# Five quarters of an MLP's second matmul by seven products in place of eight, inside the attention blocks of a Trainium2 kernel

## The chip, the cores and the metric

The kernel runs on one core of one Trainium2 chip. The metric is the device time of one execution in microseconds (us); less is better. A core has a matmul engine (PE, with a weight loader PEld), a vector engine (DVE), a scalar engine (ACT), GpSimd (POOL), DMA queues of which SP issues most, a working memory (SBUF) and eight accumulator banks (PSUM) of 128 x 512 f32 that PE writes and DVE and ACT read.

## The reference

A pre-norm transformer block with cross attention and an MLP: B = 4 sequences of L = 512 rows, D = 512, 16 heads, all in f32.

```python
q = (layer_norm(x, ln1) @ q_w + q_b)          # heads of 32
k, v = enc @ k_w + k_b, enc @ v_w + v_b
attn = softmax(where(mask, q @ k.T * scale, min))
hidden = (attn @ v) @ cproj_w + cproj_b + x
y = gelu(layer_norm(hidden, ln2) @ fc_w + fc_b)   # 512 -> 2048
out = hidden + y @ proj_w + proj_b                # 2048 -> 512
```

The change is in the last line, in `y @ proj_w` of the sequences 0 and 1.

## The kernel before

**Blocks.** Attention goes by 16 groups of four heads (w; four groups for each sequence b = w // 4) and by two halves of the query rows, which makes 32 blocks, p = 0 to 31. A block (`block`, L337) computes eight score tiles on PE (L317), which take all eight banks; DVE adds the mask and finds the minimum (`soften`, L323), ACT takes the exponential (L327), DVE transposes (L335, L360). POOL copies (L393) and DMAs on SP's queue (L398) exchange the transposed blocks between partitions (`copies`). Ahead of block p's scores, `attend` multiplies block p − 2 with V on PE (L415), and DVE divides by the sums of the rows as it takes the result out (oT, L420). The bank of that product is the last that the next eight score tiles get.

**Fills.** PE would be idle while DVE and ACT do the softmax, so each block has a list of other matmul work (`put(p, ...)`, L1115 to L1164): the projections of later groups (k, q, v), the cproj of a finished sequence, and the MLP's two matmuls of the sequences 0 and 1. `fill(0)` comes after the softens, `fill(1)` after the last transpose, each up to a budget of 3.4, and `fill(2)` issues what is left. `put` is written by hand; every engine executes its instructions in the order in which the program issues them (`manual_schedule`). `mid=` places work between the two sets of softens, and work that costs 0 (`do`) holds loads, sums and norms of other engines.

**The MLP.** fc goes by pairs of column chunks, each by seven products after Strassen and Winograd instead of eight (`fc_seven`, L634), with sums of weight blocks made on POOL (`fc_sums`, L679). proj goes by quarters (b, q): four of the 16 chunks of the inner dimension for all 512 rows. Before the change a quarter is four parts (`proj`, L701), one for each 128 rows: four matmuls 128x512 into one bank (L705), and one DVE addition of the bank to the residual tile (L709). PE shows each f32 matmul as two records. Six quarters are done this way: (0,0) to (0,3), (1,0) and (1,1). The rest of sequence 1 and the sequences 2 and 3 are done behind the blocks in `last_mlps` (L737), where proj goes by seven products already. `some(n)` takes the next items of the list `products` (L571): an fc pair counts 2, a part of proj 1. Before, (0,0) is in block 15, (0,1) in 19 and 20, (0,2) in 23 and 26, (0,3) in 27 and 28, (1,0) in 30 and 31, and (1,1) after block 31, between pieces of the last sequence's cproj (`cproj_last`, L460, itself by seven products, L479).

**Banks and buffers.** `acc_tile` (L119) hands out the eight banks in turn. An instruction that takes a bank waits for its last reader. `mlp_w` (L96) gives eight slots to the weights of fc and proj, which `load_mlp` (L582) refills as parts are done. The weights of k, q and v have two slots each in `ptt` (`kqv_w`, L111).

**After block 31** (L1184 on): `attend` of block 30, the last cproj's products q1c and q2c between parts of (1,1), stats and norms of sequence 2, POOL's row additions (`c_bias`, L437), `attend` of block 31, the rest of (1,1), then q6c, q3c, q5c and q4c, sums of proj's weights (`p_sums`, L731), and the fc pairs (1,4) to (1,7) in `last_mlps`.

Of the kernel before, what the change touches and what calls it, by code (L numbers as in the profile page):

```python
# [34 lines left out]
FIRST = 2  # L35
IN_G = (1, 3, 5, 7)
IN_XE = (25, 27, 29, 31)

BY_ROW = ((1, 1), (1, 3))
BY_ACT = ((1, 2),)  # L40
# [11 lines left out]
def xattn_block(ctx: ExitStack, tc: tile.TileContext, x, rawT, encT, mask, q_w, k_w, v_w, c_w, fc_w, p_w, vecs, rows, out):  # L52
# [6 lines left out]
    const, keep, hids, tiles, small = pools(ctx, const=1, keep=1, hids=4, tiles=4, small=4)  # L59
# [28 lines left out]

    ys = const.tile([P, 3, 2, L // 2], F32, tag="ys", name="ys")
    wsum = const.tile([P, 2, 3, 2, P], F32, tag="wsum", name="wsum")  # L90

    def k_q(w, i):
        n = w % 4 * 2 + i
# [15 lines left out]
        return ptt[:, n * D : (n + 2) * D]  # L109

    def kqv_w(w, i):  # L111
        n = 4 * i + 2 + w % 2
        return ptt[:, n * D : (n + 1) * D].rearrange("p (d f) -> p d f", d=ND)

    S = {"gelu": []}
# [92 lines left out]
            )  # L208

    def load_rn(b):  # L210
        S["rows", b] = [hids.tile([P, L], F32, tag="hid2", bufs=2, name=f"rn_{b}_{i}") for i in range(2)]
# [28 lines left out]
    def load_w(w, queue=None, names=("wk", "wq", "wv")):  # L240
# [4 lines left out]
        for i, (n, src) in enumerate((("wk", k_w), ("wq", q_w), ("wv", v_w))):  # L245
            if n in names:
                S[n, w] = kqv_w(w, i)
                (queue or Q[0]).dma_start(out=S[n, w], in_=src[:, g, :, :])

    def prep_k(w):  # L250
        b, g = divmod(w, NG)
        kT = k_q(w, 0)
        acc = acc_tile(f"acck_{w}")
        for d in range(ND):
            nc.tensor.matmul(acc, S["wk", w][:, d, :], eT[:, d, :], start=(d == 0), stop=(d == ND - 1))  # L255
        load_w(w + 2, names=("wk",))
        nc.scalar.activation(kT, acc, AF.Identity, bias=vec[:, KB + g : KB + g + 1], scale=1.0)
        S["kT", w] = kT

    def prep_q(w):  # L260
        b, g = divmod(w, NG)
        qT = k_q(w, 1)
        parts = [slice(0, L)] if w else [slice(0, 2 * P), slice(2 * P, L)]
        for c in parts:
            acc = acc_tile(f"accq_{w}_{c.start}")[:, c]
            for d in range(ND):
                nc.tensor.matmul(acc, S["wq", w][:, d, :], xT[:, d, c], start=(d == 0), stop=(d == ND - 1))  # L267
            nc.scalar.activation(qT[:, c], acc, AF.Identity, bias=qb[:, g : g + 1], scale=-scale)
        load_w(w + 2, names=("wq",))
        S["qT", w] = qT  # L270

    def prep_v(w):
# [159 lines left out]
    def load_h(b, *ts_):  # L432

        if ("xa", b) not in S:
            S["xa", b] = dram.tile([L, D], F32, tag=f"xa{b}", name=f"xa{b}")
        for t in ts_:
            if b == B - 1:  # L437

                S["h", b, t] = k_q(t // 2, t % 2)
            else:  # L440
                pool, tag, n = (tiles, "xn", 4) if not stays(b, t) else (hids, "hid2", 2) if b else (hids, "hid", 4)
                S["h", b, t] = pool.tile([P, D], F32, tag=tag, bufs=n, name=f"h_{b}_{t}")
# [93 lines left out]
    def load_hid(b, ts_):  # L536

        for t in ts_:
            if ("hid", b, t) not in S:
                S["hid", b, t] = hids.tile([P, D], F32, tag="hid", name=f"hid_{b}_{t}")  # L540
# [24 lines left out]
    def fcs(b, *cs):  # L565
        return [("fc", b, c) for c in cs]

    def pjs(b, q, *ts_):
        return [("p", b, q, t) for t in ts_ or range(NT)]

    products = fcs(0, 0, 1, 2, 3) + pjs(0, 0) + fcs(0, 4, 5) + pjs(0, 1) + fcs(0, 6, 7) + pjs(0, 2)  # L571
    products += fcs(SPLIT, 0) + pjs(0, 3) + fcs(SPLIT, 1, 2, 3) + pjs(SPLIT, 0) + pjs(SPLIT, 1)
    last_use, done = {}, 0
    for name, b, i, *_ in products:
        n = 2 if name == "fc" else FQ
# [6 lines left out]
    def load_mlp():  # L582

        while count[0] < len(weights) and (count[0] < MW or weights[count[0] - MW][3] < count[1]):
            name, b, f, _ = weights[count[0]]
            w = mlp_w(count[0])
            if name == "fc":
                w = w.rearrange("p (d f) -> p d f", d=ND)
            Q[0].dma_start(out=w, in_=fc_w[:, f, :, :] if name == "fc" else p_w[ts(f, P), :])
            S[name + "w", b, f] = w  # L590
            count[0] += 1

    NP = NF // 2
# [104 lines left out]
        count[4] += 1  # L698
        load_mlp()

    def proj(b, q, t):  # L701
        gelus(q % 2)
        acc = acc_tile(f"accp_{b}_{q}_{t}")
        for k in range(FQ):
            nc.tensor.matmul(  # L705
                acc, gT[q % 2][:, k, ts(t, P)], S["pw", b, q * FQ + k], start=(k == 0), stop=(k == FQ - 1)
            )
        h = S["hid", b, t]
        nc.vector.tensor_tensor(h, acc, h, ALU.add)  # L709
        if q == NQ - 1:  # L710
            (nc.gpsimd if b == 0 else nc.sync).dma_start(out=out[b, ts(t, P), :], in_=h)
# [25 lines left out]
    def last_mlps():  # L737
# [197 lines left out]
        for b, pairs, new in (  # L935
# [43 lines left out]

            project(b, pairs, sums, turns, middle)  # L980
            if b == SPLIT:
                S["more"] = [hids.tile([P, D], F32, tag="hid2", bufs=2, name=f"more_{n}") for n in range(2)]
                S["more"] = [m.rearrange("p (c n) -> p c n", c=NP // 2) for m in (*S["more"], row[:, 2, :])]
                to_split.extend(w_sums(5, pt[:, 2]))


# [86 lines left out]
    def some(n):  # L1073
# [4 lines left out]
        assert n == 0  # L1078
        return taken

    def hid_(b, *ts_):
        return do(lambda: load_hid(b, ts_))

# [20 lines left out]
    def put(p, *work, before=(), mid=()):  # L1104
# [48 lines left out]
    put(22, [k, q], norm(1, 0, 1), some(2), norm(1, 2, 3))  # L1153
    k15, q15, _ = A(15)
    put(23, some(1), [k15], t2, pb_(1), some(1), h_(2, 2, 3, 0, 1))
# [93 lines left out]
```

## Time and profile before

| | |
|---|---|
| median of three runs | 760.17 us (759.89 to 760.55) |
| the profiled execution, and its span | 760.67 us, 758.9 us |
| PE, DVE, ACT, POOL busy | 753.9, 613.4, 337.6, 339.7 us |
| granted clock of PE | 0.999 |

The span runs from the first instruction to the last; the execution's time has 1.8 us around it. In the rows of the profile, a group of instructions has the line of `before.py` (L705), the engine, the operation, what is written and read by the program's names, the shape, the count, busy us and mean ns of one, and the idle time ahead of them with what ended it. Rows of the timeline begin with the start in us and the duration; those of the windows with the stretch and its length, and then give each engine's busy time.

### The profile page before, as it was taken

To read this page: it belongs to the slowest core of one execution; us is meant where nothing else is said; L and a number is where in the kernel's file an instruction comes from. 1 tells how busy PE (TensorE), PEld (TensorE's weight loads), DVE (VectorE), ACT (ScalarE), POOL (GpSimd) and SP (SyncE) were. 2 spreads that over 40 slices of the span, in tenths; PEclk is the share of its full clock that TensorE was granted. 3 is DMA by queue.
4 is the path that set the end of the run, shared out by engine and by line. 5 is a ranking of instruction groups with operands and counts; after the bars stand their busy time and mean duration, and the time that the engine had idled before them with its cause. 6 is when DMAs were issued, how large, how long until landed. Compare 5 with 4: busy or idle time off the path is not lost.

```text
span 758.9 us, 13040 instructions
## 1 busy us (share of the span) xinstructions
PE 753.9 (99%) x4418; PEld 517.8 (68%) x4418; DVE 613.4 (81%) x1222; ACT 337.6 (44%) x768; POOL 339.7 (45%) x352
## 2 busy tenths in 40 slices
PE   9999999999999999999999999999999999999998
PEld 6655555567574545475454566468888899988997
DVE  3889999879995777887887989949877986956865
ACT  2566766565873574647753567501302221022200
POOL 1549447368664873244575444432050004403153
PEclk9999999999999999999999999999999999999999
DMA  9989889467897776665756867776724402046001
GB/s 329 341 255 247 207 207 257 104 199 200 220 243 229 223 231 177 184 175 129 177 133 186 214 194 193 172 227 215 260 98 135 167 26 91 30 146 214 1 15 43
DMA packets 60577, 134.59 MB, mean 177 GB/s; under 512 B 11312, under 2 KB 17072, under 8 KB 60384
## 3 DMA queue, kind: packets, MB, share of 16 engines
q1 hardware_dynamic: 58448, 126.73, 58.4%
q0 software_dynamic: 1920, 7.01, 2.7%
q8 instruction: 35, 0.57, 0.3%
q14 instruction: 30, 0.25, 0.1%
q10 hardware_dynamic: 144, 0.02, 0.0%
HBM read 69.23 MB, written 11.02 MB: 106 GB/s over the span
## 4 chain that ended last, share of the span: by engine, by line
PE 99%; POOL 0%; issue 0%; DVE 0%; DVEq 0%; POOLq 0%
PE q L646 26%; PE accp L705 11%; PE r L792 10%; PE sc L317 8%; PE av L415 8%; PE acck L255 8%; PE accq L267 8%; PE accc L455 6%; PE accv L278 5%; PE accv L298 3%; PE q1p L853 2%; PE tp L166 1%; PE warm L1044 1%; PE q3p L835 0%; PE q5p L835 0%; PE q4p L835 0%
## 5 line engine op out<-in xcount | busy, mean ns | idle before, releaser
L327 ACT ACTIVATE ptt<-ptt,mn 128x512 f32<-128x512 f32 x256 | 181.7, 711 | 142.8 <-DVE mn L323 142.8
L323 DVE CUSTOM_DVE_ANT_0 ptt<-sc,mb 128x512 f32<-128x512 f32 x256 | 160.6, 682 | 19.9 <-PE sc L317 19.8
L335 DVE STREAM_TRANSPOSE tb<-ptt 128x1024 f32<-128x1024 f32 x128 | 153.3, 1217 | 0.0
L393 POOL COPY pT<-tb 32x1088 f32<-32x1088 f32 x96 | 104.5, 1089 | 83.5 <-DVE oT L420 34.6
L705 PE MATMUL accp<-pbt,gt 128*128 128x512 f32 x192 | 85.3, 596 | 0.0
L646 PE MATMUL q<-yT,gt 128*128 128x256 f32 x320 | 78.9, 379 | 0.0
L667 ACT ACTIVATE ga<-ga,vec 128x512 f32<-128x512 f32 x40 | 26.7, 714 | 93.3 <-DVE ga L600 93.3
L646 PEld LDWEIGHTS q<-yT,gt 128*128 128x128 f32 x320 | 60.8, 190 | 8.1
L705 PEld LDWEIGHTS accp<-pbt,gt 128*128 128x128 f32 x192 | 35.9, 190 | 44.6 <-issue 39.1
L317 PE MATMUL sc<-pbt 32*128 32x512 f32 x512 | 64.7, 614 | 0.0
L646 PE MATMUL q<-ys,gt 128*128 128x256 f32 x240 | 61.6, 379 | 0.0
L255 PE MATMUL acck<-xe,ptt 128*128 128x512 f32 x128 | 59.0, 604 | 0.0
L267 PE MATMUL accq<-xe,ptt 128*128 128x512 f32 (+1 forms) x136 | 58.4, 575 | 0.0
L646 PEld LDWEIGHTS q<-ys,gt 128*128 128x128 f32 x240 | 45.7, 190 | 6.1
L600 DVE TENSOR_TENSOR ga<-q,ga 128x512 f32<-128x512 f32 (+1 forms) x60 | 36.2, 603 | 16.3 <-PE q L646 13.5
L327 ACT ACTIVATION_READ_ACCUMULATOR ptt<-ptt,mn 128x1 f32 x256 | 47.8, 187 | 0.0
L415 PE MATMUL av<-pT,v 128*32 128x256 f32 x768 | 46.4, 382 | 0.0
L267 PEld LDWEIGHTS accq<-xe,ptt 128*128 128x128 f32 x136 | 24.9, 190 | 31.4 <-issue 22.8
L255 PEld LDWEIGHTS acck<-xe,ptt 128*128 128x128 f32 x128 | 23.8, 193 | 30.8 <-issue 24.0
L317 PEld LDWEIGHTS sc<-pbt 32*128 32x128 f32 x512 | 26.9, 184 | 24.8 <-issue 16.9
L455 PE MATMUL accc<-wc,oT 128*128 128x512 f32 x96 | 42.5, 598 | 0.0
L278 PEld LDWEIGHTS accv<-ptt,xe 128*128 128x128 f32 x320 | 37.0, 192 | 4.9 <-DVE mn L323 2.7
(231 smaller groups left out, 1270.4 us busy)
## 6 DMA issues: line engine op xcount, KB each, us to landing
pT<-tb SPq DMA_DIRECT2D x288, 136.0 KB, 2.4
pbt<-p_w_dram SPq DMA_DIRECT2D x40, 256.0 KB, 3.3
gt<-ws SPq DMA_DIRECT2D x20, 512.0 KB, 3.3
gt<-tb SPq DMA_DIRECT2D x48, 136.0 KB, 3.8
xe<-tb SPq DMA_DIRECT2D x48, 136.0 KB, 2.5
pbt<-fc_w_dram SPq DMA_DIRECT2D x24, 256.0 KB, 4.7
gt<-fc_w_dram SPq DMA_DIRECT2D x20, 256.0 KB, 3.3
ptt<-k_w_dram SPq DMA_DIRECT2D x16, 256.0 KB, 4.2
```

The costliest lines, as they stand in the source:

```text
L255: nc.tensor.matmul(acc, S["wk", w][:, d, :], eT[:, d, :], start=(d == 0), stop=(d == ND - 1))
L267: nc.tensor.matmul(acc, S["wq", w][:, d, :], xT[:, d, c], start=(d == 0), stop=(d == ND - 1))
L317: nc.tensor.matmul(S["sc", w, qt][h], qT[r, ts(qt, P)], kT[r, :], start=True, stop=True)
L323: nc.vector.tensor_tensor_reduce(out=s, in0=S["sc", w, qt][h], in1=S["mb", w // NG], scale=1.0, scalar=FMAX, op0=ALU.add, op1=ALU.min, acc ...
L327: nc.scalar.activation(s, s, AF.Exp, bias=mn, scale=-1.0, accum_out=S["sums", w][:, qt, h : h + 1])
L335: nc.vector.transpose(tv[:, qt % 2, 2 * k : 2 * k + 2], S["ps", w, qt, k])
L393: nc.gpsimd.tensor_copy(pT[ts(i, HD), i], tb[ts(i, HD), i])
L415: nc.tensor.matmul(av[ts(h, HD), : 2 * P].rearrange(shape, **kw), v[:, t, ts(h, HD)], p[t][h], start=(t == 0), stop=(t == NT - 1),)
L455: nc.tensor.matmul(acc, S["oT", b][:, g, ts(t, P)], wc[:, g, :], start=(g == 0), stop=(g == NG - 1))
L646: nc.tensor.matmul(o, x[:, k], y[:, k], start=(k == 0), stop=(k == 1))
L705: nc.tensor.matmul(acc, gT[q % 2][:, k, ts(t, P)], S["pw", b, q * FQ + k], start=(k == 0), stop=(k == FQ - 1))
L792: nc.tensor.matmul(r, x[:, c], w[:, c], start=(c == 0), stop=(c == NP // 2 - 1))
```

## The change

For five of the six quarters, the product of a quarter (512 rows by 512 inner, times 512 inner by 512 columns) is cut into 2 x 2 blocks a (activations) and w (weights) of 256 each, and done by seven products of blocks, each of four matmuls 128x256 in a bank of its own. (1,0), in `WHOLE`, keeps the old form (`proj_whole`).

- `proj_sums` makes four sums ahead of the products: x = a21 + a22 and y = w12 − w11 (in free slots of `ptt`), a21 = a11 − a21 and w12 = w22 − w12 in place. They run on POOL, except that x and y are DVE's for (1,1). `pre(b, q)` places it.
- Part 0: products q1, q5, q2 (q1, q2, q5 for (1,1)); ACT copies q1 into w11, and q5 into a11 except for the quarters in `FOUND5`; four more sums on POOL; DVE joins q2 (and q1 for the quarter in `FOUND1`, and q5 twice for those in `FOUND5`) to the residual.
- Part 1: q7, q6; two DVE additions out of the banks, and the joins of what they give on POOL: three for (0,0), six for (0,1) and (0,2), four for (0,3) and (1,1).
- Part 2: q3, q4, and a DVE join of each into a quarter of the residual into which POOL has joined a sum before.

So a quarter has three parts and not four, and they are placed anew: (0,0) in block 15, its part 0 ahead of the V product; (0,1) in 19 and 20; (0,2) in 23, 25 and 26; (0,3) in 27, 28 and 29, mixed with fc pairs; (1,1) after block 31 as before. Block 30's list is reversed, so that the part of (1,0) stands ahead of the fc pair. Two stats move from block 20 to 19, a load of residual rows from the end of block 30 to its middle. From group 10 on the weights of k and q have one slot, which frees two slots of `ptt`. The tiles of the residual become two fixed tiles, `hid4` and `hid2`, and the output rows of sequence 0 are stored after (0,3)'s part 2, all four together.

```diff
+SINGLE = 10
+WHOLE = ((1, 0),)
+FOUND1, FOUND5 = ((0, 0),), ((0, 0), (0, 3), (1, 1))
...
-        n = 4 * i + 2 + w % 2
+        n = 4 * i + 2 + (w % 2 if i == 2 or w < SINGLE else 0)
...
+    def next_w(w, name):
+        if w != SINGLE - 1:
+            load_w(w + (2 if w < SINGLE else 1), names=(name,))
...
+    def proj_sums(b, q):
+
+        gelus(q % 2)
+        a11, a21, a12, a22, w11, w12, w21, w22, x, y = proj_blocks(b, q)
+        e = nc.vector if b else nc.gpsimd
+        add(e, x, a21, a22)
+        sub(y, w12, w11, e)
+        sub(a21, a11, a21, nc.gpsimd)
+        sub(w12, w22, w12, nc.gpsimd)
...
+        def product(name, a, w):
+            o = acc_half(f"{name}_{b}_{q}")
+            for t in range(2):
+                for k in range(2):
+                    nc.tensor.matmul(o[:, t], a[:, k, ts(t, P)], w[:, k], start=(k == 0), stop=(k == 1))
+            return o
+
+        def join(engine, i, j, src):
+            h = hid2 if b and i == 0 else hid4[:, 2 * i : 2 * i + 2]
+            h = h[:, :, ts(j, HL)]
+            add(engine, h, src, h)
+
+        if part == 0:
+            q1 = product("q1j", a11, w11)
+            nc.scalar.copy(w11, q1)
+            if (b, q) in FOUND1:
+                join(nc.vector, 0, 0, q1)
+            if b:
+                q2 = product("q2j", a12, w21)
+            q5 = product("q5j", x, y)
+            sub(x, x, a11, nc.gpsimd)
+            sub(y, w22, y, nc.gpsimd)
+            if (b, q) in FOUND5:
+                join(nc.vector, 0, 1, q5)
+                join(nc.vector, 1, 1, q5)
+            else:
+                nc.scalar.copy(a11, q5)
+            if not b:
+                q2 = product("q2j", a12, w21)
+            join(nc.vector, 0, 0, q2)
+            sub(a12, a12, x, nc.gpsimd)
+            sub(w21, w21, y, nc.gpsimd)
+        elif part == 1:
+            q7 = product("q7j", a21, w12)
+            q6 = product("q6j", x, y)
+            add(nc.vector, y, q6, w11)
+            add(nc.vector, a21, q7, y)
+            late = () if (b, q) in FOUND1 else ((0, 0, w11),)
+            if (b, q) not in FOUND5:
+                late += (0, 1, a11), (1, 1, a11)
+            for i, j, src in (*late, (0, 1, y), (1, 0, a21), (1, 1, a21)):
+                join(nc.gpsimd, i, j, src)
+        else:
+            q3 = product("q3j", a12, w22)
+            join(nc.vector, 0, 1, q3)
+            q4 = product("q4j", a22, w21)
+            join(nc.vector, 1, 0, q4)
+            if q == NQ - 1:
+                for t in range(NT):
+                    (nc.gpsimd if b == 0 else nc.sync).dma_start(out=out[b, ts(t, P), :], in_=S["hid", b, t])
...
-    put(14, [q], some(2), x1)
-    put(15, x2[:1], V(10), x2[1:2], do(lambda: load_raw(3)), some(2), do(lambda: store_rn(3)), some(1),
-        do(lambda: load_rn(3)), some(1))
+    put(14, [q], some(2), x1, pre(0, 0))
+    put(15, some(1), x2[:1], V(10), x2[1:2], do(lambda: load_raw(3)), some(1), do(lambda: store_rn(3)), some(1),
+        do(lambda: load_rn(3)))
...
-    put(18, [q], some(2), [k])
+    put(18, [q], some(2), [k], pre(0, 1))
     k, q, v = A(13)
-    put(19, some(2), [k])
-    put(20, [q], stat(1, 0, 1), some(2))
+    put(19, [k], some(1), stat(1, 0, 1))
+    put(20, [q], some(2))
...
-    put(25, c[:3])
-    put(26, c[3:], do(lambda: attend(12, 0)), some(2))
-    put(27, some(3))
+    put(25, c[:3], some(1))
+    put(26, c[3:], do(lambda: attend(12, 0)), some(1))
+    put(27, some(3), mid=pre(0, 3))
     put(28, some(3))
-    put(29, some(4))
-    put(30, some(3), hid_(1, 2, 3))
-    put(31, some(3))
+    put(29, some(3))
+    put(30, some(3)[::-1], mid=hid_(1, 2, 3))
+    put(31, some(3), pre(1, 1))
...
-    run(some(2) + do(c[1]) + stat(2, 2, 3) + rs(2) + cb(B - 1) + norm(2, 0, 1) + some(1) + do(c[2]))
+    run(some(1) + do(c[1]) + stat(2, 2, 3) + rs(2) + cb(B - 1) + norm(2, 0, 1) + some(1) + do(c[2]))
```

More of the change, by code (lines that the diff above doesn't have):

```diff
@@ L210, in load_rn @@
     def load_rn(b):
-        S["rows", b] = [hids.tile([P, L], F32, tag="hid2", bufs=2, name=f"rn_{b}_{i}") for i in range(2)]
+        S["rows", b] = [hid2[:, i] for i in range(2)]
         for i in range(2):
@@ L440, in load_h @@
             else:
-                pool, tag, n = (tiles, "xn", 4) if not stays(b, t) else (hids, "hid2", 2) if b else (hids, "hid", 4)
-                S["h", b, t] = pool.tile([P, D], F32, tag=tag, bufs=n, name=f"h_{b}_{t}")
+                S["h", b, t] = (
+                    (hid2 if b else hid4)[:, t] if stays(b, t)
+                    else tiles.tile([P, D], F32, tag="xn", name=f"h_{b}_{t}")
+                )
             Q[0].dma_start(out=S["h", b, t], in_=x[b, ts(t, P), :])
@@ L699, in fc_by_pair, with proj_blocks, proj_whole @@
         load_mlp()
-    def proj(b, q, t):
+    def proj_blocks(b, q):
+        g = gT[q % 2]
+        w = [pbt[:, n * D : (n + 2) * D].rearrange("p (k f) -> p k f", k=2) for n in
+             (S["pw", b, q * FQ + k] for k in (0, 2))]
+        a11, a21, a12, a22 = (g[:, 2 * k : 2 * k + 2, ts(i, HL)] for k in range(2) for i in range(2))
+        w11, w12, w21, w22 = (w[k][:, :, ts(j, HL)] for k in range(2) for j in range(2))
+        x, y = (
+            ptt[:, n * D : (n + 1) * D].rearrange("p (k l) -> p k l", k=2)
+            for n in ((10, 11) if (b, q) == (0, NQ - 1) else (3, 7))
+        )
+        return a11, a21, a12, a22, w11, w12, w21, w22, x, y
+    def proj_sums(b, q):
[6 more added lines that the diff above has]
+        sub(w12, w22, w12, nc.gpsimd)
+    def proj_whole(b, q, t):
         gelus(q % 2)
@@ L981, in last_mlps @@
             if b == SPLIT:
-                S["more"] = [hids.tile([P, D], F32, tag="hid2", bufs=2, name=f"more_{n}") for n in range(2)]
-                S["more"] = [m.rearrange("p (c n) -> p c n", c=NP // 2) for m in (*S["more"], row[:, 2, :])]
+                S["more"] = [
+                    m.rearrange("p (c n) -> p c n", c=NP // 2) for m in (hid2[:, 0], hid2[:, 1], row[:, 2, :])
+                ]
                 to_split.extend(w_sums(5, pt[:, 2]))
```

37 lines of the change are left out of this document (24 added, 13 removed).

## The prediction

> **What bounds the kernel now.** I read the page's head first, then its chain of waits, then the costliest groups, and after that stretches of the trace.
>
> ```profile
> span 758.9 us, 13040 instructions
> PE 753.9 (99%) x4418; PEld 517.8 (68%) x4418; DVE 613.4 (81%) x1222; ACT 337.6 (44%) x768; POOL 339.7 (45%) x352
> PE 99%; POOL 0%; issue 0%; DVE 0%; DVEq 0%; POOLq 0%
> L705 PE MATMUL accp<-pbt,gt 128*128 128x512 f32 x192 | 85.3, 596 | 0.0
> ```
>
> The matmul engine (PE) is busy from end to end and 99% of the chain that ended last runs over it, so matmul time taken away counts until another engine is late. DVE, at 81%, is the next one. L705 is the work that the change shortens: 192 records for six quarters of proj, 32 a quarter. Busy time overstates matmuls, whose records overlap; starts in the timeline give the true pace.
>
> ```profile
> 228.08 13.90 PE L705 MATMUL accp<-pbt,gt 128*128 128x512 f32 x32
> 241.91 1.94 PE L415 MATMUL av<-pT,v 128*32 128x256 f32 x32
> ...
> 512.04 1.89 PE L479 MATMUL q3c<-wc,oTt 128*128 128x256 f32 x8
> ...
> 517.22 1.89 PE L646 MATMUL q<-yT,gt 128*128 128x256 f32 x8
> ```
>
> The first two rows (start, duration) frame one whole quarter, block 15's: 241.91 − 228.08 = 13.83 us. The others are products exactly like the new ones (four matmuls 128x256 in a bank), in the last cproj: the three from q3c on take 517.22 − 512.04 = 5.18, so 1.73 each.
>
> **What is saved.** Seven products are 7 × 1.73 = 12.09 us, 13.83 − 12.09 = 1.74 less than a quarter. Five quarters: −8.7 us, if PE waits for nothing new. The sixth quarter, (1,0), stays whole.
>
> **What is added.** By the diff, POOL gets 61 tensor_tensor operations of 128x512 (11, 14, 14, 12 and 10 for the quarters in order). DVE has 34 of them where the five quarters had 20 joins at L709. ACT gets a copy of q1 in each, and of q5 in two.
>
> ```profile
> L426 POOL TENSOR_TENSOR h<-h,row 128x512 f32<-128x512 f32 x18 | 22.6, 1283 | 0.9 <-DMA h<-x_dram 0.7
> L600 POOL TENSOR_TENSOR pbt<-wct,pbt 128x512 f32<-128x512 f32 x3 | 4.6, 1568 | 8.1 <-DVE wct L600 8.1
> L426 POOL TENSOR_TENSOR hl<-hl,row 128x512 f32<-128x512 f32 x4 | 6.6, 1675 | 30.5 <-issue 30.5
> L709 DVE TENSOR_TENSOR h<-accp,h 128x512 f32<-128x512 f32 x20 | 13.5, 679 | 12.1 <-PE accp L705 12.1
> L494 ACT COPY wct<-q1c 128x512 f32<-128x512 f32 x1 | 0.6, 586 | 10.1 <-issue 10.1
> ```
>
> So POOL gets 61 × 1.28 = 78 us, 102 at the dearest row (1.675). DVE gets 14 × 0.68 = 9.5, ACT 7 × 0.59 = 4. ACT, at 44%, hides its copies: the next work that wants that bank or block is a product later. What the others cost depends on the ends of the blocks, because there DVE's last work in a block sits ahead of its oT product (L420), and the next block's eighth score tile takes the bank that oT frees.
>
> **How late oT may be.** The end of block 27 and the end of block 28:
>
> ```profile
> 427.96 0.65 DVE L600 TENSOR_TENSOR gt<-q,p 128x512 f32<-128x512 f32 x1
> 428.72 1.95 DVE L600 TENSOR_TENSOR gt<-q,gt 128x512 f32<-128x512 f32 x3
> 430.43 2.34 PE L317 MATMUL sc<-pbt 32*128 32x512 f32 x16
> 430.58 0.68 DVE L709 TENSOR_TENSOR h<-accp,h 128x512 f32<-128x512 f32 x1
> 431.17 0.42 DVE L420 TENSOR_TENSOR oT<-av,pT 128x256 f32<-128x256 f32 x1
> 432.70 0.70 PE L705 MATMUL accp<-pbt,gt 128*128 128x512 f32 x1
> ...
> 445.06 2.00 PE L317 MATMUL sc<-pbt 32*128 32x512 f32 x16
> 446.99 1.99 PE L646 MATMUL q<-yT,pbt 128*128 128x256 f32 x8
> ```
>
> In block 29 the fill follows the scores by 446.99 − 445.06 = 1.93. In block 28 oT ended at 431.59, 1.16 after the scores began, and the fill came 2.27 after them: 0.34 late. So a block is late by what oT's end is past the start of the scores plus about 0.82. Block 27 began at 416.96: DVE's fixed work (eight softens, five transposes) ended 427.96 − 416.96 = 11.0 into it, the additions of an fc pair took 430.58 − 427.96 = 2.62, a join 0.59, oT 0.42. With this DVE clock a block is late by 11.0 + additions + 0.42 − PE's length − 0.82. PE's lengths and busy times:
>
> ```profile
> core 0: us, PE busy (x) PEld busy (x) DVE busy (x) ACT busy (x) POOL busy (x), PEclk, DMA share, GB/s
> 219.14:243.77 24.63, 24.63 (x116) 13.86 (x113) 16.68 (x38) 12.20 (x26) 12.86 (x17) 1.00 0.77 224
> 295.34:309.63 14.29, 14.29 (x76) 6.26 (x72) 11.51 (x25) 9.83 (x22) 8.31 (x10) 1.00 0.67 174
> 309.63:323.92 14.29, 14.29 (x76) 6.26 (x72) 13.04 (x29) 7.75 (x19) 4.35 (x4) 1.00 0.77 198
> 388.14:400.56 12.42, 12.42 (x44) 5.31 (x40) 11.52 (x25) 6.27 (x17) 8.58 (x8) 1.00 0.64 157
> 416.96:430.43 13.47, 13.47 (x89) 8.54 (x85) 12.49 (x27) 6.54 (x18) 2.43 (x4) 1.00 0.77 211
> 461.13:474.74 13.61, 13.61 (x89) 8.69 (x85) 13.16 (x28) 10.05 (x23) 4.89 (x7) 1.00 0.61 162
> ```
>
> These are blocks 15, 19, 20, 25, 27 and 30.
>
> **Quarter (0,0), block 15.** DVE has room (16.68 of 24.63 us), POOL has little:
>
> ```profile
> 219.82 4.47 POOL L393 COPY pT<-tb 32x1088 f32<-32x1088 f32 x4 [4.50 <-DMA pbt<-fc_w_dram]
> ...
> 229.36 2.49 POOL L309 TENSOR_TENSOR v<-v,row 128x512 f32<-128x512 f32 x2 [0.56 <-ACT v L302]
> ...
> 233.62 0.19 POOL L140 TENSOR_SCALAR rn<-rn 128x4 f32<-128x4 f32 x1
> ```
>
> The four sums ahead of the products run at the end of block 14, and push the copies back by about 1 us. In the queue then stand the copies with the fc sums and two DMA issues (219.82 to 229.36 before, less the 0.56 of waiting: 9.0), four new sums (5.1), v_bias (2.5), the norm's row (1.9) and the first two joins (2.6): 220.8 + 9.0 + 5.1 + 2.5 + 1.9 + 2.6 = 241.9. Only then can DVE do q4's join (0.6), the mask (0.4) and oT (0.42): 243.4, against scores that begin at 243.77 − 1.74 = 242.03. Late by 1.35 − 0.82 = 0.5, up to 0.7 with one more wait on DVE; I take 0.65. Net −1.1 (bounds −1.7, nothing late, and −0.2, all copies and sums at 1.4).
>
> **(0,1), blocks 19 and 20.** Part 0 (5.2) takes the place of two old parts (7.0) in block 19, PE's length becomes 12.5, and the two stats move there: the 13.04 − 11.51 = 1.5 us by which block 20's DVE exceeds block 19's. DVE: 11.0 + 0.6 + 1.5 + 0.42 − 12.5 − 0.82 = 0.2; I take 0.3, and 0.2 for block 20's joins behind POOL's six. Net −1.2 (−1.7 to −0.6).
>
> **(0,2), blocks 23, 25 and 26.** A single part in each; DVE stands at 11.52 of 12.42 in block 25, which becomes 3.5 longer for 1.2 of additions. I charge 0.2. Net −1.5 (−1.7 to −1.0).
>
> **(0,3), blocks 27 to 30.** Block 27: q5's sums wait on POOL, and three joins (1.8) replace one: 11.0 + 2.62 + 1.8 + 0.42 against 13.47 − 3.5 + 5.2 = 15.2, 0.0 late (0.3 if q5 waits for its y). Block 28 (an fc pair, q7 and q6, two additions): 11.0 + 2.62 + 1.22 + 0.42 = 15.26 against 13.4: 1.0 late, 1.15 with its late start. Block 29, with q3 and q4 ahead of the fc pair: the same sum, less what it begins late; 0.8. Block 30: 0.2, as before. Together 2.25 with 0.1 of q5's wait, where the old blocks lost 0.34 + 0.2 and about 0.1. Net −1.74 + 1.6 = −0.1 (−1.3 to +0.8).
>
> **(1,1), after block 31.** Here DVE's queue is long, and in the changed order of banks the second product of fc pair (1,4) takes the bank of q3c, so it waits for q3c's join.
>
> ```profile
> 512.31 0.69 DVE L600 TENSOR_TENSOR wct<-q6c,wct 128x512 f32<-128x512 f32 x1 [1.10 <-PE q6c L479]
> ...
> 514.97 0.73 DVE L597 TENSOR_TENSOR ptt<-pbt 128x512 f32<-128x512 f32 x1
> 515.73 1.64 DVE L597 TENSOR_TENSOR ptt<-pbt,ptt 128x512 f32<-128x512 f32 x1
> 517.29 1.75 DVE L597 TENSOR_TENSOR pbt<-pbt 128x512 f32<-128x512 f32 x1
> 518.97 0.68 DVE L597 TENSOR_TENSOR ptt<-pbt,ptt 128x512 f32<-128x512 f32 x1
> 519.57 0.68 DVE L600 TENSOR_TENSOR pbt<-q3c,pbt 128x512 f32<-128x512 f32 x1
> ...
> 500.49 5.26 POOL L426 TENSOR_TENSOR pbt<-pbt,row 128x512 f32<-128x512 f32 x4 [0.30 <-DMA pbt<-x_dram]
> 513.87 4.62 POOL L600 TENSOR_TENSOR pbt<-wct,pbt 128x512 f32<-128x512 f32 x3 [8.12 <-DVE wct L600]
> ```
>
> Before, that product followed the first one without a wait, at 517.22 + 0.86 = 518.08 (half of the 1.73). After, DVE's string begins 1.74 earlier with q6c, and q3c's join ends at 520.25 − 1.74 = 518.5: 0.4 after the old time. It is later still where the string starts late: q4's join stands ahead of it and waits for POOL's third join, behind the four row adds (5.26). Row adds end between 504 and 505.75; with three joins (3.84) that is 507.9 to 509.6, against q6c's end at 510.6 and two DVE joins in between: 0 to 0.3, to 1.2 with a slow POOL. I take 0.45: the quarter ends 0.85 later than before (0.3 earlier, if the sums get cheaper, to 1.8 later). This quarter loses.
>
> Sum: −1.1 − 1.2 − 1.5 − 0.1 + 0.85 = −3.05. Added bounds in quadrature (0.7, 0.6, 0.4, 1.0, 1.1) are 1.8.
>
> The first two middle sums, 515.73 and 517.29, took 1.64 and 1.75 while POOL's joins ran (513.87 to 518.49); those at 514.97 and 518.97 took 0.73 and 0.68. [...]
>
> **Elsewhere, nothing.** The k and q weights with a single buffer are loaded one block later, still blocks ahead of their use; PE has no wait for them in the chain, so I put it at 0 (if a load of the kind came late, a block would lose under 1 us). The fixed hid tiles change no size. Output stores of b=0 are four at once, far from the end.
>
> **Rivals.**
> - Full gain: every wait is hidden. 760.67 − 8.7 = 752.0. For it: PE is 99% of the chain. Against it: oT's rows and block 30's 13.16 of 13.61 on DVE. Chance 0.08.
> - POOL sets the ends of blocks (slower). Every q3 and q4 join on DVE waits for a POOL join into the same quadrant, and oT is behind it. If POOL's operations go at 1.57 to 1.68, as in two rows above, in place of 1.28, each of the 43 sums and joins that stand after a first product adds 0.3 to 0.4. It decides from 0.11 on each (43 × 0.11 = 4.7, which turns −3.05 into +1.65); at half the dear price, 0.17, it gives 760.67 − 3.05 + 7.3 = 764.9. For it: POOL's full queue in block 15. Against it: the 18 row adds at 1.283, most of them beside softens. Chance 0.16.
> - The tail eats the gain. All four DVE sums ahead of q3c's join run into POOL's longer queue and take the 1.7 that two of them take now, so q3c's join comes 2 × 1.0 later: 760.67 − 3.05 + 2.0 = 759.6. For it: the rows of 1.64 and 1.75. Against it: 514.97 ran beside POOL too, at 0.73. Chance 0.20. [...]
>
> **How the numbers follow.** My forecast has 0.56. The profiled execution is 760.67 (span 758.9 and 1.8 around it), 0.5 above the median of 760.17. So 760.67 − 3.05 = 757.6, and for the median 757.1; its own range is 755.3 to 758.9. A change under 0.2% (1.5 us) can't be told from none here. Faster: 0.88 of 0.56, and 0.08, is 0.57. Same: the rest of the forecast (0.07) and the tail's rival (0.19) are 0.26. Slower: 0.17. For 8 in 10 I leave out the full gain and the dear end of POOL's rival: 754.8 to 762.2.
>
> **What would show it.** Products at 1.73 each and L705 down to 32 records confirm the gain. Scores of block 29 that take about 1.1 longer, DVE busy to the end of blocks 27 to 30, and q26 of pair (1,4) starting right at the end of q3c's join confirm the losses. POOL rows of the new sums near 1.28 speak against the second rival, near 1.6 for it. I am wrong if PE shows gaps inside the products of a quarter (a late sum or bank), or none at all at the ends of the blocks.

## The result, and the profile after

The changed kernel takes 771.73 us (median of four, 769.44 to 772.78), the kernel before in the same runs 760.36: ratio 1.0146, interval 1.0119 to 1.0172. It is slower by 11.4 us, where I forecast 3 us less. The profiled execution took 772.78 us, span 771.0, 12.1 more than before.

The head of its page, two lines of its slices, and the waits of PE (us in all, times, longest):

```profile
PE 756.0 (98%) x4538; PEld 543.5 (70%) x4538; DVE 630.7 (82%) x1236; ACT 340.9 (44%) x775; POOL 419.6 (54%) x413
...
PE   9999999999999999899999999987999999999998
...
PEclk9999999999998999999999999999999999999999
```
```profile
PE q L658 <- DVE pbt L612: 2.7, 1, 2.7
PE q6c L490 <- DVE oTt L609: 2.6, 1, 2.6
PE q5c L490 <- DVE wct L612: 2.0, 1, 2.0
PE av L424 <- DMA ptt<-k_w_dram: 2.0, 1, 2.0
...
PE sc L326 <- DVE hid L612: 0.7, 1, 0.7
```

PE has new waits, and its clock dips in the slice from 231 to 251 us. The chain of waits is now 87% on PE, where it was 99%. Where the 12.1 us are is read from windows that begin and end at the first score of a block (15 to 17, 18 to 20, 21 and 22, 23 to 26, 27 to 30, the rest), first of the kernel before, then of the changed one:

```profile
219.14:278.39 59.25, 59.25 (x288) 31.64 (x284) 42.42 (x92) 32.77 (x71) 41.94 (x45) 1.00 0.80 235
278.39:323.92 45.53, 45.52 (x240) 22.53 (x236) 37.28 (x81) 25.26 (x60) 17.01 (x18) 1.00 0.69 182
323.92:357.76 33.84, 33.84 (x204) 23.17 (x200) 27.09 (x58) 20.97 (x50) 15.71 (x18) 1.00 0.60 149
357.76:416.96 59.20, 59.20 (x324) 29.66 (x321) 49.30 (x105) 33.44 (x81) 36.04 (x34) 1.00 0.64 163
416.96:474.74 57.78, 57.78 (x349) 36.08 (x345) 53.10 (x112) 37.26 (x84) 26.30 (x32) 1.00 0.73 200
474.74:758.90 284.16, 280.51 (x1636) 242.60 (x1632) 216.58 (x364) 50.35 (x101) 80.67 (x71) 1.00 0.39 122
```
```profile
219.46:283.87 64.41, 63.64 (x313) 38.01 (x309) 45.25 (x96) 33.44 (x72) 51.66 (x53) 0.95 0.74 217
283.87:331.46 47.59, 45.58 (x264) 27.82 (x260) 37.48 (x81) 25.99 (x62) 33.22 (x32) 0.96 0.65 166
331.46:365.52 34.06, 34.06 (x204) 23.41 (x201) 27.68 (x59) 20.98 (x50) 21.79 (x23) 1.00 0.66 174
365.52:423.78 58.26, 58.26 (x348) 34.56 (x344) 49.92 (x106) 34.37 (x83) 45.51 (x42) 1.00 0.64 169
423.78:480.98 57.20, 57.20 (x373) 41.02 (x369) 54.92 (x116) 37.36 (x85) 45.73 (x47) 1.00 0.75 202
480.98:771.00 290.02, 279.17 (x1660) 246.57 (x1656) 227.84 (x368) 51.24 (x102) 95.79 (x80) 1.00 0.37 119
```

By the second column: +5.16, +2.06, +0.22, −0.94, −0.58 and +5.86, with 0.32 ahead of block 15. Two quarters gain, (0,2) and (0,3); (0,0), (0,1) and (1,1) lose 13.1 us between them. The clock (after the engines) is 0.95 and 0.96 in the first two stretches. Inside them two short windows lie at half of it:

```profile
246.10:253.00 6.90, 6.79 (x10) 2.51 (x10) 6.90 (x17) 4.34 (x12) 6.06 (x7) 0.51 0.94 285
314.40:317.80 3.40, 3.40 (x32) 1.65 (x27) 0.42 (x1) 1.51 (x2) 1.70 (x2) 0.50 0.00 0
```

**Block 15 and 16.** The timeline of the changed kernel, ACT, then POOL, then DVE, then PE (start, duration, idle before):

```profile
234.70 0.40 ACT L365 COPY rr<-rsum 128x256 f32<-128x256 f32 x1 [5.43 <-DVE rsum L363]
235.12 1.28 ACT L679 ACT_TABLE_LOAD   x1
236.42 1.33 ACT L679 ACTIVATE gt<-gt,vec 128x512 f32<-128x512 f32 x2
237.66 1.17 ACT L311 COPY v<-accv 128x256 f32<-128x256 f32 x4
...
238.63 2.50 POOL L318 TENSOR_TENSOR v<-v,row 128x512 f32<-128x512 f32 x2 [4.09 <-ACT v L311]
...
246.96 0.41 DVE L429 TENSOR_TENSOR oT<-av,pT 128x256 f32<-128x256 f32 x1
...
245.08 4.41 PE L326 MATMUL sc<-pbt 32*128 32x512 f32 x6 [0.66 <-DVE hid L612]
249.42 5.45 PE L264 MATMUL acck<-xe,ptt 128*128 128x512 f32 x8
```

V now comes in the second fill, behind three products of (0,0), and ends 5.5 us later on PE than before (233.74 and 228.24). ACT's copies of v therefore stand in ACT's queue behind the copy of rr, a table load and the gelu, and POOL stands idle for 4.09 us until they are done. So v_bias begins at 238.63, 9 us later than before; POOL's joins stand behind it, and oT ends at 247.4, 4.9 after the scores began. The clock is at half from 246.1, and the projection of k takes 5.45 where eight such records take 3.6 elsewhere. Block 16 is 23.70 long, 6.8 more than before.

**Behind block 31.** DVE's sums for the last cproj and the norm between them, first before the change:

```profile
491.59 0.69 DVE L597 TENSOR_TENSOR wct<-wc,wct 128x512 f32<-128x512 f32 x1
...
500.22 1.95 DVE L157 TENSOR_SCALAR h<-h,mv,rs 128x512 f32<-128x512 f32 x2 [1.51 <-POOL rs L143]
...
507.37 0.69 DVE L597 TENSOR_TENSOR oTt<-oT 128x512 f32<-128x512 f32 x1
```

and after it, with one of POOL's sums beside them and POOL's row adds:

```profile
499.28 0.68 DVE L609 TENSOR_TENSOR wct<-wc 128x512 f32<-128x512 f32 x1
499.99 1.64 DVE L609 TENSOR_TENSOR wct<-wc,wct 128x512 f32<-128x512 f32 x1
...
504.91 1.75 DVE L609 TENSOR_TENSOR oT<-oT 128x512 f32<-128x512 f32 x1
...
511.51 2.90 DVE L162 TENSOR_SCALAR h<-h,mv,rs 128x512 f32<-128x512 f32 x2 [1.44 <-POOL rs L148]
...
516.10 1.20 DVE L609 TENSOR_TENSOR oTt<-oT 128x512 f32<-128x512 f32 x1
517.34 1.64 DVE L609 TENSOR_TENSOR oTt<-oT,oTt 128x512 f32<-128x512 f32 x1
...
501.05 1.71 POOL L609 TENSOR_TENSOR ptt<-ptt,gt 128x512 f32<-128x512 f32 x1
...
511.46 5.29 POOL L435 TENSOR_TENSOR pbt<-pbt,row 128x512 f32<-128x512 f32 x4
```

In the changed kernel most of these sums, with both inputs in SBUF, take 1.64 to 1.75 us on DVE, and 1.71 on POOL, as long as both run. Counted from block 31's first score (474.74 before, 480.98 after), the norm begins 5.0 us later than before, and oTt's first sum, for which q6c waits, ends 3.0 us later. PE waits 2.6, 2.0 and 2.7 us for this string and its followers.

### The profile page after: what moved, and what is told of

Its sections match the earlier page's. It is cut to its first block, busy times and chain, and to the rows that moved or that the text cites. A ratio compares the mean times of both kernels' runs of the same rounds, so it can differ in the third digit from the quotient of the medians.

```text
span 771.0 us, 13400 instructions
## 1 busy us (share of the span) xinstructions
PE 756.0 (98%) x4538; PEld 543.5 (70%) x4538; DVE 630.7 (82%) x1236; ACT 340.9 (44%) x775; POOL 419.6 (54%) x413
## 4 chain that ended last, share of the span: by engine, by line
PE 87%; DVE 4%; POOL 2%; DMA 2%; SPq 2%; issue 1%; ACT 1%; DVEq 0%; POOLq 0%; ACTq 0%
PE q L658 24%; PE r L877 10%; PE sc L326 8%; PE acck L264 8%; PE accq L276 7%; PE av L424 7%; PE accc L466 5%; PE accv L287 5%; PE q1p L938 2%; PE accv L307 2%; SPq L407 2%; PE tp L171 1%; POOL hid L612 1%; DMA pT<-tb 1%; PE q3j L759 1%
## 5 line engine op out<-in xcount | busy, mean ns | idle before, releaser
L326 PE MATMUL sc<-pbt 32*128 32x512 f32 x512 | 71.4, 625 | 0.8 <-DVE hid L612 0.7
L658 PEld LDWEIGHTS q<-yT,gt 128*128 128x128 f32 x320 | 60.6, 190 | 11.2 <-DVE pbt L612 3.1
L264 PE MATMUL acck<-xe,ptt 128*128 128x512 f32 x128 | 61.2, 622 | 0.0
L326 PEld LDWEIGHTS sc<-pbt 32*128 32x128 f32 x512 | 29.1, 188 | 29.3 <-issue 17.5
L318 POOL TENSOR_TENSOR v<-v,row 128x512 f32<-128x512 f32 x16 | 20.3, 1279 | 45.7 <-ACT v L292 33.6
L435 POOL TENSOR_TENSOR hid<-hid,row 128x512 f32<-128x512 f32 x18 | 23.5, 1331 | 36.2 <-DMA hid<-xa 36.2
```

Of the source, the lines that this page charges most:

```text
L326: nc.tensor.matmul(S["sc", w, qt][h], qT[r, ts(qt, P)], kT[r, :], start=True, stop=True)
L658: nc.tensor.matmul(o, x[:, k], y[:, k], start=(k == 0), stop=(k == 1))
```

## The experiments

On the chips on which the next kernels ran, some blocks ahead of block 15 took longer in some executions: block 15 starts between 218.8 and 223.5 us, and the kernel before took 761.6 to 762.4. In block 14 of three_undone, the last pT transfer landed 4.7 us after its issue, 2.5 in the kernel before. So I compare lengths of stretches between scores in the traces, and give the times beside them.

**1. The three losses undone, one by one and together.**

v_first puts V ahead of part 0 in block 15:

```diff
-    put(15, some(1), x2[:1], V(10), x2[1:2], do(lambda: load_raw(3)), some(1), do(lambda: store_rn(3)), some(1),
+    put(15, x2[:1], V(10), some(1), x2[1:2], do(lambda: load_raw(3)), some(1), do(lambda: store_rn(3)), some(1),
```

tail_whole has (1,1) in `WHOLE` too, its parts placed as in the kernel before; q01_whole has (0,1) in it, with blocks 18 to 20 as before; three_undone is all three (its edit in part):

```diff
-WHOLE = ((1, 0),)
+WHOLE = ((1, 0), (1, 1), (0, 1))
...
-    put(19, [k], some(1), stat(1, 0, 1))
-    put(20, [q], some(2))
+    put(19, some(2), [k])
+    put(20, [q], stat(1, 0, 1), some(2))
...
```

> Block 15's list as before: the V product first, part 0 of (0,0) behind it. Theory ACT's order: with V in the second fill, ACT's copies of v stand behind the copy of rr and the gelu, so POOL's v_bias began at 238.6 in place of 229.4, and POOL's joins, DVE's joins and oT came 4 us late behind it. With V first, v_bias is back near 229 to 231, block 16 falls from 23.7 to 17.0 to 17.6 us, no stretch of it has a granted clock under 0.95, and the time falls by 5.5 to 6.5 us. Rival, POOL's amount: its eleven new operations alone make the block late; then block 16 stays above 21 us and the time falls by under 2.

> (1,1) back to four parts with one DVE join each, behind block 31 as before. Theory sums beside POOL: PE's three idle stretches of that tail (2.6, 2.0 and 2.7 us) come from DVE sums that take 1.65 to 1.75 us beside POOL's new ones, so without (1,1)'s seven products all three are gone, and the time falls by 5.5 to 6.3 us, all of it behind block 31. Rival, arrears: the tail is late because blocks 15 to 30 leave DVE and POOL behind; then one or two of the idle stretches stay and the time falls by under 3.

> (0,1) back to four parts, two in block 19 and two in 20, the stats back in 20. Theory short block: block 19 with three products in place of two parts is shorter than the exchange of the transposed block takes from one oT to the next product with V (12.2 us), so PE waited 2.0 us for the last pT transfer and ran at half clock for some 3 us after; with whole parts blocks 19 and 20 return to 14.3 each, and the time falls by 1.9 to 2.5 us. Rival: the single buffer of k's weights holds up SP's queue; then the wait ahead of block 20 stays, and the time rises or falls by under 1.

> All three of the above together; (0,0), (0,2) and (0,3) keep their seven products. If the three losses are each a thing of its place, they add up: 771.7 - 6.0 - 5.9 - 2.2 = 757.6, which is 2.6 to 2.8 us below the kernel before, by (0,0) -1.1, (0,2) -0.9 and (0,3) -0.6. Rival, one cause for all (POOL's queue is full wherever seven products are): (0,0), (0,2) and (0,3) lose too once the others don't hide it, and the time is 760 or more.

| us | time (before) | blocks 15–17 | 18–20 | 27–30 | from 31 on |
|---|---|---|---|---|---|
| before | 760.36 | 59.25 | 45.53 | 57.78 | 284.16 |
| after | 771.73 | 64.41 | 47.59 | 57.20 | 290.02 |
| v_first | 772.31 (761.67) | 58.98 | 50.23 | 57.19 | 289.98 |
| tail_whole | 766.81 (761.67) | 65.05 | 47.92 | 57.19 | 283.88 |
| q01_whole | 774.39 (761.67) | 64.95 | 45.63 | 57.19 | 291.61 |
| three_undone | 760.28 (761.67) | 58.99 | 45.53 | 57.19 | 283.95 |

Each stretch answers to its own edit: 5.4, 6.1 and 2.0 us. With V first, v_bias starts 10.2 us into block 15 (232.83 − 222.61), just as in the kernel before (229.36 − 219.14), and block 16 takes 18.27, a little over what was expected; 1.4 us stay lost there. V first moves the product on PE as well as ACT's copies, so the run shows that V's place costs the 5.4 us; that ACT's queue is the link is read from POOL's idle 4.09 us above. In q01_whole k's weights still have one buffer and PE's wait ahead of block 20 is gone, so the single buffer isn't its cause.

The whole times follow less well. By the ratios to the kernel before (1.0063, where the changed kernel has 1.0146), tail_whole's fell by 6.3 us, as expected. Those of v_first and q01_whole did not fall, against the expectation. In v_first the wait ahead of block 20 was 3.79 us, the V product and the scores behind it took 3.64 and 2.78 us (1.93 and 2.00 in late_store, below), and blocks 18 to 20 took 2.6 us more than in the first profile; in q01_whole the tail took 1.6 us more, and the profiled execution's mean granted clock was 0.988 (0.993 for the changed kernel). The three together come to a ratio of 0.998 (0.9961 to 0.9998), about 1.5 us and half of what was expected: in the trace, (0,0) is worth 0.26 us in blocks 15 to 17 and not 1.1, (0,2) 0.66 in blocks 23 to 26 (58.54, before 59.20) and not 0.9. So the losses are three things and not one, and V's place in block 15 is the first.

**2. What stretches the tail.**

only_tail is v_first with (0,1) whole. tail_fill is that with each of POOL's six sums for (1,1) changed like this one:

```diff
-            sub(x, x, a11, nc.gpsimd)
+            nc.gpsimd.memset(x, 0.0) if b else sub(x, x, a11, nc.gpsimd)
```

and tail_dve is only_tail with the four sums of part 0 like this:

```diff
-            sub(x, x, a11, nc.gpsimd)
+            sub(x, x, a11, nc.vector if b else nc.gpsimd)
```

> V first in block 15 and (0,1) whole, so of the three losses only that behind block 31 is left; the base for the next two. If the tail's loss is its own, this kernel takes 5.5 to 6.3 us more than the one with all three undone (on the same day's kernel before: about 4.5 us above it), PE has idle stretches ahead of q6c, q5c or q3c, and the fc pair (1,4), together 6 to 8 us, and DVE's sums for the last cproj take 1.6 to 1.75 us beside POOL's sums. If it was arrears from earlier blocks, the idle stretches sum to less than 4.

> As the last one, but the two sums ahead of (1,1)'s products and the four between them, POOL's, are fills with zero into the same blocks: POOL writes there and reads nothing, so sequence 1's output lacks those sums. Theory sums beside POOL: DVE's first five sums of the last cproj fall from 1.65-1.75 to about 0.7 us each, DVE's string is 4 us earlier, the idle stretches of PE lose 3 to 4.5 us and so does the time; DVE's sums that run beside POOL's row adds and joins stay dear. Rival, POOL's joins behind the row adds (what I predicted): DVE's sums are dear for another reason, and PE's idle changes by under 1.5 us.

> As the first one, but (1,1)'s four sums between the products are DVE's and not POOL's: 2.8 us more work on DVE, 5 to 7 us less on POOL. Theory sums beside POOL: DVE's five sums and the four new ones go at 0.7 to 0.75, which gives back more than it costs, and the time falls by 0.5 to 2 us. Rival, DVE has too much work there whatever POOL does: the time rises by 2 to 3 us.

They took 765.01, 762.16 and 767.58 us beside 761.64 for the kernel before; from block 31 on 290.39, 284.69 and 289.05. In only_tail PE idles 5.7 us ahead of q6c and q3c, near the 6 to 8 expected, so the tail's loss is its own; its time, 3.4 us over the kernel before, is under the 4.5 expected. DVE's sums in the timeline of tail_fill, POOL writing zeros beside them:

```profile
491.81 0.68 DVE L609 TENSOR_TENSOR wct<-wc 128x512 f32<-128x512 f32 x1
492.53 0.69 DVE L609 TENSOR_TENSOR wct<-wc,wct 128x512 f32<-128x512 f32 x1
...
494.34 0.68 DVE L609 TENSOR_TENSOR oT<-oT 128x512 f32<-128x512 f32 x1
...
505.86 1.64 DVE L609 TENSOR_TENSOR oTt<-oT,oTt 128x512 f32<-128x512 f32 x1
```

All five sums are at 0.7, and the stretch loses 5.7 of the 6.2 us by which it was over the kernel before: DVE's string and the row adds behind it start 4 us earlier, PE's waits of 2.6 and 3.1 become one of 2.0, and q3c and q5c take 1.99 and 1.89 us in place of 2.84 and 2.77, at a mean granted clock of 1.000 in place of 0.996. By the medians it is 2.85, under the 3 to 4.5 expected. The oTt sums, beside POOL's row adds, stay dear, as expected. The fills are also shorter than the sums (0.53 us a piece in the trace, against 1.7), so the run takes away POOL's reading and two thirds of its time at once; some of DVE's sums did run beside a fill, at 0.68 and 0.69. That POOL's reading alone makes the sums dear is therefore likely and not shown by itself. Moving four sums to DVE brought the first five to 0.68, but for the second at 1.64, and the stretch down by 1.3 in the one trace. The median of its times rose by 2.6 us (764.92 to 771.83 in its runs), as the rival said; so it is no remedy as it stands, and what the longer executions lost is open.

**3. The wait ahead of block 20.**

late_store is v_first with the stores of the last fc pair of sequence 0 held back to block 20:

```diff
-                nc.gpsimd.dma_start(out=sums_dram[c, :, :3], in_=s)
-                nc.gpsimd.dma_start(out=sums_dram[c, :, 3], in_=y[:, :2])
+                def stores(c=c, s=s, y=y):
+                    nc.gpsimd.dma_start(out=sums_dram[c, :, :3], in_=s)
+                    nc.gpsimd.dma_start(out=sums_dram[c, :, 3], in_=y[:, :2])
...
+        if p == 20:
+            S["stores"]()
```

> The kernel with V first, and (0,1) in its seven products, but POOL's two stores of weight sums (512 KB) in block 19 are issued a block later. Theory transfers: the last pT transfers of block 19's exchange landed 4 to 5 us after their issue because they ran beside these stores, and 2.4 us after it in the kernel before; with the stores away the wait ahead of block 20 falls from 2.0-3.8 to at most 1 us, with no stretch of half clock in blocks 19 and 20. Rival, short block: twelve issues on SP (7.8 to 9 us) and 2.4 us of landing are by themselves more than the block's 10.7 us from oT to the next product, and a wait of 1.3 us or more stays.

768.33 us (before 761.64). PE's wait and SP's queue in late_store:

```profile
PE av L424 <- DMA ptt<-k_w_dram: 1.3, 1, 1.3
```
```profile
299.02 9.05 SPq L407 DMA_DIRECT2D pT<-tb  x12
308.18 0.51 SPq L253 DMA_DIRECT2D ptt<-k_w_dram  x1
```

The row names the load of k's weights, which uses the semaphore of an earlier pT transfer; PE waits for the last pT transfer. In late_store that one landed at 310.11, PE went on at 310.45, and the load landed only at 310.90. In the changed kernel these three are 313.29, 313.63 and 314.14.

The wait falls from 3.79 in v_first to 1.27, the V product and the scores behind it are back at 1.93 and 2.00 (3.64 and 2.78 in v_first), and blocks 18 to 20 take 45.32 (50.23 in v_first). Both theories hold in part: the stores delayed the landing (2.6 us after the issue here, 5.0 in v_first), and twelve issues in 9 us still end too late for this block. Even so (0,1) gains only 0.2.

**4. What is left in block 16.**

stats_early is three_undone with:

```diff
-    put(15, x2[:1], V(10), some(1), x2[1:2], do(lambda: load_raw(3)), some(1), do(lambda: store_rn(3)), some(1),
+    put(15, x2[:2], V(10), do(lambda: load_raw(3)), some(1), do(lambda: store_rn(3)), some(1), do(lambda: load_rn(3)),
...
```

> As the kernel with all three undone ((0,1) and (1,1) whole, V first), and in block 15 the last two stats and the norm's row stand ahead of V, where POOL and DVE have room. Theory: what block 16 still loses there (18.28 in place of 16.9 us) is POOL's joins that start 1.3 us late, behind the norm's row, whose stats DVE does between joins; with them ahead, POOL's joins come about 1.3 us earlier, block 16 falls to 16.9-17.3 us and the time to 1.0-1.4 us below the one with all three undone, 2 to 3.5 us below the kernel before (ratio 0.9955 to 0.9975). Rival: POOL's sum of work up to the joins sets them, not its order; block 16 stays at 18 or more.

762.10 us (before 761.84; ratio 1.0004, 0.9985 to 1.0022). Block 16 is 16.90 as expected, but block 15 grew from 22.98 to 25.76: q6 waits 2.5 us for POOL's sum y, which now comes behind the norm's row. The loss moved and grew: the two blocks take 42.66 us, where three_undone has 41.26. Neither expectation came whole. Block 16 did not stay at 18, as the rival had it, and the time did not fall. POOL also stands idle for 2.04 us there, until DVE's stats are done for the norm's row, so this run doesn't show that POOL's sum of work alone sets the loss.

**5. What a wait costs.**

Both are the kernel before, with this eight (idle_3) or fourteen times (idle_6) ahead of block 16's oT:

```diff
+                    nc.vector.tensor_scalar(S["mb", 2], m8, 0.0, FMAX, ALU.is_equal, ALU.mult)
```

> The kernel before, with the mask of block 16 made eight times more on DVE ahead of oT (8 x 0.42 = 3.4 us): the ninth score tile's bank comes late and PE waits some 3 us there, nothing else changed. Theory half clock: PE's clock is halved for 3.4 us (or twice that) after such a wait, so the block takes 3.1 us for the wait and 1 to 2 more for slow matmuls, 21 to 22.5 in place of 16.9. Rival, a wait costs itself: the granted clock stays 1.00 and block 16 takes 19.8 to 20.2.

> The same with fourteen times (5.9 us). Theory half clock: at least 6.8 us at half clock, 3 us or more on top of the wait of 5.5: block 16 takes 25 or more in place of 16.9. Rival, a wait costs itself: 22.2 to 22.8.

The waits were longer than I meant, because the repeated masks also waited for the next mask's transfer (3.66 us in idle_3, 4.85 in idle_6). PE in idle_3, then the clock in a window of idle_3 and of idle_6:

```profile
253.00 2.07 PE L317 MATMUL sc<-pbt 32*128 32x512 f32 x2 [5.05 <-DVE oT L420]
255.00 5.45 PE L255 MATMUL acck<-xe,ptt 128*128 128x512 f32 x8
260.29 3.60 PE L267 MATMUL accq<-xe,ptt 128*128 128x512 f32 x8
```
```profile
251.70:258.60 6.90, 5.60 (x7) 2.04 (x8) 6.87 (x17) 4.34 (x12) 5.37 (x5) 0.51 0.62 141
```
```profile
250.30:260.50 10.20, 5.01 (x6) 1.95 (x7) 9.86 (x26) 4.34 (x12) 4.78 (x5) 0.50 0.36 82
```

Block 16 takes 25.75 with a wait of 5.05, 8.85 more than 16.90; and 29.45 with a wait of 9.01, 12.55 more. So 3.5 to 3.8 us come on top of either wait, in windows with a clock of 0.51 and 0.50: behind the wait the last two records of the scores take 2.07 us in both runs, and k's projection 5.45 and 5.18, where it takes 3.60 at full clock. That a wait costs itself alone is ruled out for these two. The whole times rose by 11.2 and 12.5.

**6. The two quarters that gain, alone, and the order of banks.**

two_left has blocks 14 to 20, and the work behind block 31, placed as before (its edit in part); two_shifted adds the second edit to it.

```diff
-WHOLE = ((1, 0),)
+WHOLE = ((1, 0), (0, 0), (0, 1), (1, 1))
...
-    put(14, [q], some(2), x1)
+    put(14, [q], some(2), x1, do(lambda: [acc_tile(f"skip_{n}") for n in range(3)]))
```

> Only (0,2) and (0,3) keep seven products; (0,0), (0,1) and (1,1) are whole, with the order of blocks 14 to 20 as in the kernel before. By the lengths of blocks 23 to 30 in the changed kernel's trace, (0,2) is worth -0.9 us and (0,3) -0.6 there, with no stretch of half clock: 1.5 us below the kernel before (ratio 0.998), about the time of the kernel with three undone. Rival: seven products pay nowhere, because POOL and DVE give the gain back in later blocks; then the time is that of the kernel before or more.

> The kernel with two quarters left, and three accumulator tiles taken and not used at the end of block 14, which turns the order of banks by three from there on. With two left, the second product of fc pair (1,4) waited 2.05 us for DVE's join of q3c, whose bank it takes; with the three turned it takes another one. Theory bank order: that wait is gone, the stretch from block 31's scores to the end falls from 286.0 us to 284.0-284.3, as in the kernel before, blocks 23 to 30 keep their 1.5 us, and the time is 1.3 to 1.7 us below the kernel before (ratio 0.998). Rival, DVE's sums set the pace there whatever the bank: the wait moves to the next product of the pair and the stretch stays above 285.5.

two_left: 762.95 us (before 762.36; ratio 1.001, 0.9987 to 1.0034). Blocks 23 to 30 keep their 1.5 us, but the rest takes 285.97 in place of 284.16:

```profile
517.41 1.03 PE L658 MATMUL q<-yT,gt 128*128 128x256 f32 x4
520.48 1.13 PE L658 MATMUL q<-yT,gt 128*128 128x256 f32 x4 [2.05 <-DVE pbt L612]
```

two_shifted: 760.90 (before 762.00; 0.999, 0.9974 to 1.0006), from block 31 on 283.96, with no wait there:

```profile
519.31 1.89 PE L658 MATMUL q<-yT,gt 128*128 128x256 f32 x8
```

The wait ahead of the second product of pair (1,4) is the banks' order, shown by turning that alone. The interval of two_shifted reaches over 1, so three_undone, at 0.998 (0.9961 to 0.9998), is the one version here that the runs put below the kernel before, by 0.2%.

## Why the prediction was wrong

Of the 15.2 us between the forecast and the trace, (0,0) makes 6.3, (1,1) 5.0 and (0,1) 3.3.

- **The saving in PE** was right: products go at 1.73 us, and block 15 fell by 1.65 (24.63 to 22.98).
- **(0,0), −1.1 forecast, +5.2 measured.** The step that failed is "the copies with the fc sums ..., four new sums, v_bias": I let v_bias start when POOL came to it, at 234.9 by the sum, and wrote that ACT "hides its copies". It started at 238.63. V had been moved past the rr copy and the gelu in ACT's queue, and I had not followed that queue. By my own rule, oT at 4.9 past the scores makes a block about 4.1 late; the other 2.7 of block 16's 6.8 go with the half clock (k's projection alone took 5.45 in place of 3.60). With V first, 1.4 is late where I had 0.65.
- **(0,1), −1.2 against +2.1.** I followed DVE and POOL's joins, not the exchange: PE came to the next product with V 10.6 us after oT began (301.01 to 311.6), and the last pT transfer landed 12.3 after it. "Elsewhere, nothing" left out POOL's stores beside the transfers.
- **(0,2), −1.5 against −0.9, and (0,3), −0.1 against −0.6**: the rule of how late oT may be held, but the sizes were off. PE's work behind block 26's scores comes 0.70 late, where I charged 0.2 for block 25; behind the scores of 29 and 30 it is 1.04 and 0.49 late (1.15 and 0.8 in the sum), behind those of 28 and 31 not at all. That the two quarters together came out at −1.5, with −1.6 forecast, is luck: the two errors cancel.
- **(1,1), +0.85 against +5.9.** The wait on q3c's bank was there (2.7), and the product starts at 530.39, as q3c's join ends at 530.34; but I kept the durations of before for all of DVE's string. My third rival had dearer sums beside POOL, and the wrong place: the two sums that it stretched stayed at 0.73 and 0.68, and some ten others took longer than such work alone, from (1,1)'s own x and y (1.20 and 1.57) and the first sums of cproj to the norm (2.90, before 1.95) and the oTt sums (1.20 to 1.75, before 0.69). In tail_fill, where POOL writes zeros in place of its six sums, the first five of cproj's took 0.68 to 0.69. I had the two dear rows of before (1.64 and 1.75), and applied them to four sums only.
- **Waits priced at their length.** No term had the half clock. It came to 1.6 us behind the wait ahead of block 20, where the V product and the scores took 5.43 us in place of 3.80, and to 3.5 to 3.8 in experiment 5.
- The second rival (POOL at 1.6 everywhere) had the wrong price: POOL's new sums took 1.27 to 1.29 in the traces of blocks 15 and 19, and 1.7 in the tail only.
- **Three signs that I named came all the same**: L705's form has 32 records left, block 29's scores take 3.04 us, 1.04 longer, and no product waits inside a quarter. They tested the terms that I had, not the queues that I had left out.

## What to carry to other kernels

Where a step is moved, follow each engine's own queue for what now stands ahead of its copies, ACT's too, and not only the engine that is busiest. Where two engines both get sums over working memory, price them at their rows from places where both ran (here 1.64 to 1.75 us on DVE, 0.68 to 0.69 without), not at their means. Price a wait on PE with and without the half clock behind it (here it added 1.6 us behind a wait of 2.01 and 3.5 to 3.8 behind 5.05 and 9.01), and where tiles turn through a ring of banks, ask which tile follows which once their number changes.

## What the runs showed of the hardware

The half clock comes in stretches. In the changed kernel's trace they are 6.83 us (from 246.14) and 3.41 us long (from 314.41), in idle_3 and idle_6 windows of 6.90 and 10.20 us have a clock of 0.51 and 0.50. The same wait is dear in one place and cheap in another: behind the 2.01 us ahead of block 20 of the changed kernel the V product took 2.94, behind 2.12 ahead of block 15 of three_undone 1.93. The two starts in the changed kernel's trace lie 68.27 us apart, 20 times 3.413, and the two lengths are two times and one time that. That its clock is set anew every 3.413 us is an estimate of mine from these three numbers; no run tested it. Four windows of that length, three of the changed kernel, at whole multiples of it from 314.41, and one of only_tail (after the length, PE's busy time):

```profile
311.00:314.41 3.41, 1.40 (x19) 0.82 (x22) 3.01 (x7) 3.38 (x6) 3.41 (x4) 1.00 0.75 227
515.80:519.21 3.41, 1.76 (x8) 1.61 (x9) 3.34 (x4) 0.00 (x0) 3.41 (x3) 1.00 0.02 5
526.04:529.45 3.41, 1.69 (x8) 1.14 (x6) 3.41 (x3) 0.37 (x1) 2.54 (x2) 1.00 0.29 118
```
```profile
514.56:517.97 3.41, 0.99 (x5) 0.89 (x6) 2.82 (x5) 0.00 (x0) 2.87 (x2) 1.00 0.79 290
```

In the first of them PE is idle for 2.01 us, and the 3.41 us behind it are at a clock of 0.50. In the last it is idle for 2.42, and q3c, which starts 0.99 us ahead of the window's end, and q5c take 2.84 and 2.77 us in place of the 1.99 and 1.89 of tail_fill. In the other two it is idle for 1.65 and 1.72, since waits of 2.58 and 2.66 fell on two windows each, and the clock stays at 1.00. Block 16 of the changed kernel doesn't go by such lengths: the window ahead of its half clock, 242.73 to 246.14, has 0.66 us of idle. So these runs don't show how much idle time halves the clock, and none of them moved a wait against the windows.

The half clock alone doesn't explain why the changed kernel's times spread over 3.3 us where the kernel before spreads over 0.8: its executions of 772.66 and 769.44 us have the same mean clock, 0.996.
